# Sums of two weight slots in one operation and in place, six plain slots, a fourth weight buffer and a new order

## The chip, the cores and the metric

The kernel runs on 1 core of one Trainium2 chip. The metric is device microseconds of one execution. Engines: PE (TensorE, the matmuls; PEld is its weight load), DVE (VectorE), ACT (ScalarE), POOL (GpSimd), SP (SyncE, which here issues almost all DMAs).

## What is computed

A gated feed-forward block, for 4 sequences of 1024 tokens of width 512, with 2048 hidden rows and a down projection with weights of three values:

```python
scale = cond @ norm_w.T + 1.0
ms = jnp.mean(x * x, axis=-1, keepdims=True)
h = x * (scale[:, None, :] * jax.lax.rsqrt(ms + EPS))
u = h @ up_w.T
val, gate = jnp.split(u, 2, axis=-1)
h = val * jax.nn.gelu(gate, approximate=False)
hq = act_quant(h)          # 8 bits by row
wq = weight_quant(down_w)  # -1, 0, 1 by one scale
return hq @ wq.T + x
```

## The kernel before

**Tiles.** A batch is one sequence; its 2048 hidden rows are 16 slots of 128 rows of value and 128 of gate, and its 1024 tokens are two halves of 512. The f32 product of the up projection is made of f16: weights and activations are each split into a high and a low part, and high by high, high by low and low by high are summed in PSUM. A matmul is 128x128 by 128x512.

**Two forms of a slot.** A plain slot (`plain`, `plain_half`, and `plain_first` for the first half of slot 0) is value and gate, two halves of tokens, four blocks of 128 of the width, three terms: 48 matmuls. The other form (`slot` and `product`) takes the weights of a slot as 2x2 blocks, a11 and a12 of the gate, a21 and a22 of the value, 128x256 each, and the activations likewise, and makes seven products of six matmuls (Winograd's form of Strassen's): 42. It needs sums of the weights' blocks, and DVE and ACT add the products up (L868 to L907). In batches 1 to 3 all slots have this form. In batch 0 `SEVEN` says from which slot on: slots 0 to 6 are plain, 7 to 15 by products.

**The weights.** `w_load(j)` loads the f32 rows of slot j into a buffer of the large array H that `W_SLOT` names; in batch 0's later part three buffers (14, 12, 13) take turns. `w_range` and `w_scale` (L474, L476) scale them by powers of two. `w_rows` casts a high part (ACT, L499) and a low part (DVE, L500) of f16 and turns them by DMA. `s_sums(j)` makes the four sums of blocks (L526 to L529) into a place of their own, `sf`, which is H's buffer 17; POOL does this for the first slots and DVE for the later ones. `s_high` (L539) and `s_low` (L543) cast the sums, and `s_spill` writes all parts of the slot to `s_dram`.

**Batches 1 to 3** read the parts back into a ring of slots (SXY) by `s_load_x` and `s_load_y`: plain loads (L570) where batch 0 had turned all parts before it spilled them, and loads that transpose (L568) for the slots below `SEVEN`. `PLACE` says where each of a slot's seven parts stands.

**The start.** Two loads of x (L1130) bring the first 512 tokens. `first_sum` makes sums of squares (L1143 on ACT, L1145 on DVE), `first_root` their inverse roots, `first_scale` scales the rows (L1162, L1164), PE turns them into four banks of PSUM (`first_turn`, L1169: po_97, po_101, po_102 and A_91), and `first_high` (L1173 on ACT) and `first_low` (L1177 on DVE) make the high and low parts of x. The first weights are turned on PE as well (L484), into E_103 (one half of the rows), E_98 and then po_101 and po_102, and cast by L509 to L521. `keep_warm` (L1185) fills PE with matmuls that nobody reads. Squares go into junk buffers; the first one goes into the buffer of slot 0's value weights (`wn(0)`), whose load waits for it.

**What sets the order.** The functions only record steps. `Book.emit` issues them in the order of `ORDER`, a packed table of all steps that was planned beforehand; each engine runs its steps in that order, and waits at semaphores. The table holds one order for all five engines, SP's queue of DMAs among them.

Of the kernel before, what the change touches and what calls it, by code (L numbers as in the profile page):

```python
# [13 lines left out]
F16 = mybir.dt.float16  # L14
# [9 lines left out]
P = 128  # L24
# [12 lines left out]
PLACE = {4: 0, 5: 1, 6: 2, 2: 3, 3: 4, 0: 5, 1: 6}  # L37
# [35 lines left out]
class Book:  # L73
# [29 lines left out]
    'c-mcB2Y40b5}i#j1V|{UKnOh`AWcA2qzQsb5wU><MHEGv=(8fI=tD(CY@nz#dj~A2s7O&kB%vcBAU&az0MfGa&YAz;oA~zol6&vo',  # L103
    '-M`G7Idf+A#!DsnM^9)C*`bx>u%6Phq`Dl@Ku+s16{#k>HAxcXfTl~nhFS&Jq)T*^l@rQ8kt(tZW9;?c)sX`IORGsaDaP1)HAfEV',
    'Z(3REW41MVj#R)k+jR%t9oNm;1fP#;MOh`aFw#D)D?jN4_$EmL`AgHJBK|)o4{A1MN|ZPWb#&bL;&j=iTQR~(O_iVZLitnAmNU9b',
    '<D{od)C$r<j$v-@W4$()PV$3}kpbEocNJsC19}jjpVBiJbq7|yQw#Mn*`!4nvyaThnS3oL9c8k%kYVzgay7}=MI3fi9u^xUZ`#g_',
    'Gz0TA#5V!fbp$r-CLifVvKVt$k}}vq7Iu0Bdq0G|<>2!lN(&`PBRLDUEwWF;<tx2Zrfa6G*E+Z|Q@+rivJAUujBoSwJ$**H$_Shj',
    '`3@^7(gsqfH6>M+W8Ru_P4H~U`5WSFh&^u8suB-tEWkQn!ajK1CU59KsU=fz)nP3o_2h3|jFtX_I}X5x4ROab{ahv~eKtwjVr4f<',
    '6P&#l?=F^0qzzV(fsu-&hu$q$;4Bd%u+)CNL%xCKI8PRA`K)fl4tirQfnTn{4vu3LPvUivc9!>Wwk@ukti2=~))CpFyRp*sc7Kk1',
    'ua{t#T<<MF#uCldmB2)j+%8kGFCsDrqw>l|*z+K)Bn@krXzTnA_wsmJ9?%~0rS=Qn5Bd41{w^JKr?vvND@rq<HNtQ@P&){#_}0$U',  # L110
    '2X-C_{;_)|N<H8zMHXp$e3~NH!&^P&79EORUo5}l`d8&Hl|aKHtqt6+z?l|7UYIV;v5xMr2uJB83xMWdl&}1&2n1HZtSR_zqcl*i',
    ';CEp6sHR)|?6terNGoMrr2wh*Y@I!2pmxCLclCOF`pcgci=;$&&mAlDT+G-T{#gsZo@3|Q%agW)TGB@U126un^ifq<w!O5I&-8Y9',
    'U4ZqUFyC+5M$SiEFEAfv0v+Fg2g(E0uVTg&87H$eA9!}N(HC{#y-~25$Z<njBlxk0EJbuQm#VTyS7|ex&6fGVYzBDYGrbbH-LG8f',
    '^Lh`ydrt2~RJ4`Ru<mM20spka+PcC=1sJsr)<jlF!@7R8dC!9dGhnkCwuTS&S{qm71HBHPc~v#U#5Vm0c6k;%K82Yd1?~h9w+2!F',
# [12 lines left out]
    '`N0kP4$gFzHQ_nIOdTNgbrU{MN8C4;l^TYhY2Sd^hdUw4sOcQ<Qioh9V*K)ju@FaI0&d@L`R#W@ri=EDng=eb<aUM(5UruE#d0}Z',
    'odJul#{WbptqiH7TZrmY^UgY>%pmQ(u5fV>WfFeQ56cAH)5C~Y&ag=n;7uMIfzcw*W<0h*K?$<cUoi!+0`D4G_9n0Gv)6V&KN0WL',
    '`Dv`>05atVSm_tg2#vvDE{l?tm_z^8TKMCg35ahhx&qUE9N{=n&MZ+8df;yR*7+<2ag*%r=u{!E+O4bww&>e>BSyRk49}7F0eu-B',
    '6O6Zb=nZ!`Pw<ab0{`|P$IJ<@!19ZsB*@$!A=edRuIL~_ocF#$Y*Sem=^lL_t7A5-59@6}G{W*wgQ*h5cf5QjotgKgFIcRMIP5(o',  # L130
    'S85(+`6s3i$miX`r*C1EJQ6LwmV$SYk>pZbmx|RaKwO<4yW<3EizpWp2P5=F8Hg<2-(q1Nl>TDFQCH-_ESVuU+m+K0#R9~<1@%-0',
    'vB=|h=+#kBwhm>qhf_M640n&pW2Pt>8$)z5xIGUZ%rh$$K<l=YXY_vQ4IWr;@myetEKsti$dAyhwZU`Ff=}s#(B=K{_bs%?-?9C_',
    'j~q$0SVl4|KgA<+5Q{bCaUE+&p}z-#VVLioU3g@I^%C*Q6}W@ku}i55oK-l+7-ZX~h8A~@>Z+q$q>Js2_fU;)(s8EsiOn1JZJga~',
    '*vSV6bKN40@C3_4laY}&Tjuys%A0<<2i&m4W)z%Bv6{1nc`+Mn5!fLcx`j2b)0JBh4|_c}({!I<s;y~oSLI%%pWs|Ya96y|AlUhv',
    'R>QD@;&BVCM=ob(ZKHq3Fi{S;?IErbOVT3dMDT|@nC(yLquBdOb$fL7K{cWEf_NyotNoR$p_-{SE{Db>4q1J3ohLoh6A3pU%WO49',
    'As<yUPNClx7I%mnswZ`-uu7#`A~M{H#a2e;OLV%*KH2!<Pg8f?(fRtT<xR2tahq;IMMaGF(CL~MxcZhereYPFQCIW6>%d@{xZB0e',
    'UU2SqWxnOeWbbMc)jI;6BEgGFl`%|TwljA@0iQsmufeDfLko<uv*V!P>tRO$Y(!MwtTRf26|2}{48j;lg&mTly6%c`lvqYz3>*E8',
    'wO6%@;FM--uCRJYK%Q-`D{W20Rx9~jnR$<BCbGEG8dMb`pB0~qyB6O~^=o%p#OeCW5#i0`-$y55ymfX_jI8A97U&Mt$?nLq%vQtf',
# [1614 lines left out]
```

## Time and profile before

| | us |
|---|---|
| median of 3 runs | 717.09 (716.98 to 717.37) |
| the profiled execution | 716.0 |
| its span in the profile | 714.2 |
| PE busy | 707.6 |
| DVE busy | 527.8 |
| ACT busy | 432.8 |
| POOL busy | 144.2 |

The span goes from the first instruction to the last; 1.8 us lie around it. The profile's views give busy time of an engine by line and by stretch, waits with the engine that ended them, the chain of work that ended last, and for DMAs the time from issue to landing. A row such as `PE A L791 x12` is twelve matmuls in a row from line 791 into the PSUM tile A. Lines are those of the kernel before; after the change the same code stands 1 line earlier up to L430, and up to 11 lines later from L500 on (L791 becomes L802, L1177 becomes L1188, L570 becomes L581).

### The profile page before, as it was taken

To read this page: it belongs to the slowest core of one execution; us is meant where nothing else is said; L and a number is where in the kernel's file an instruction comes from. 1 tells how busy PE (TensorE), PEld (TensorE's weight loads), DVE (VectorE), ACT (ScalarE), POOL (GpSimd) and SP (SyncE) were. 2 spreads that over 40 slices of the span, in tenths; PEclk is the share of its full clock that TensorE was granted. 3 is DMA by queue.
4 is the path that set the end of the run, shared out by engine and by line. 5 is a ranking of instruction groups with operands and counts; after the bars stand their busy time and mean duration, and the time that the engine had idled before them with its cause. 6 is when DMAs were issued, how large, how long until landed. Compare 5 with 4: busy or idle time off the path is not lost.

```text
span 714.2 us, 10170 instructions
## 1 busy us (share of the span) xinstructions
PE 707.6 (99%) x3642; PEld 357.5 (50%) x3642; DVE 527.8 (74%) x837; ACT 432.8 (61%) x739; POOL 144.2 (20%) x161
## 2 busy tenths in 40 slices
PE   8999999999999999999999999999999999999998
PEld 4544444444444446655444455555444444444854
DVE  7968899998478896767659756775638846547895
ACT  5688889886578675654547476453434565334362
POOL 3675521120200005440202032800110000000010
PEclk9999999999999999999999999999999999999999
DMA  8778999999899973777345754566344354433324
GB/s 291 237 223 221 232 230 275 230 190 228 260 212 238 248 238 92 231 165 152 99 133 121 153 142 123 155 171 120 72 137 159 82 132 98 110 118 111 120 87 165
DMA packets 182943, 121.46 MB, mean 170 GB/s; under 512 B 144598, under 2 KB 150503, under 8 KB 182892
## 3 DMA queue, kind: packets, MB, share of 16 engines
q1 hardware_dynamic: 182346, 120.68, 64.8%
q8 instruction: 28, 0.46, 0.2%
q14 instruction: 23, 0.19, 0.1%
q10 hardware_dynamic: 546, 0.13, 0.1%
HBM read 63.73 MB, written 23.11 MB: 122 GB/s over the span
## 4 chain that ended last, share of the span: by engine, by line
PE 98%; DVE 2%; issue 0%
PE A L791 41%; PE E L791 21%; PE B L791 10%; PE po L1077 9%; PE E L806 5%; PE A L806 3%; PE B L806 2%; PE po L1027 2%; PE E L1027 1%; PE B L1077 1%; PE A L1027 1%; PE A L1185 1%; DVE wam L447 0%; PE E L1077 0%; PE A L1077 0%; PE B L1027 0%
## 5 line engine op out<-in xcount | busy, mean ns | idle before, releaser
L791 PEld LDWEIGHTS <-SXY 128*128 128x128 f16 x2226 | 217.7, 98 | 247.7 <-issue 0.2
L791 PE MATMUL A<-R,SXY 128*128 128x512 f16 x1200 | 291.0, 379 | 0.0
L791 PE MATMUL E<-R,SXY 128*128 128x512 f16 x600 | 152.5, 379 | 0.0
L923 ACT ACTIVATE gm<-H 128x512 f32<-128x512 f32 x120 | 75.6, 630 | 56.0 <-DVE R L924 45.3
L924 DVE TENSOR_TENSOR R<-R,gm 128x512 f32<-128x512 f32 x120 | 85.7, 714 | 29.1 <-ACT gm L923 28.5
L868 DVE TENSOR_TENSOR E<-A,v 128x512 f32<-128x512 f32 x57 | 39.7, 697 | 60.6 <-PE A L791 51.6
L791 PE MATMUL B<-R,SXY 128*128 128x512 f16 x318 | 82.7, 379 | 0.0
L1004 DVE TENSOR_TENSOR H<-H,am 128x1024 int8<-128x1024 f32 x64 | 77.0, 1222 | 0.0
L1009 ACT CAST R<-H 128x1024 bf16<-128x1024 int8 x64 | 65.3, 1042 | 18.1 <-DVE H L1004 17.9
L942 POOL PARTITION_ALL_REDUCE am<-R x8 | 15.6, 1950 | 256.8 <-DVE R L924 256.8
L1077 PE MATMUL po<-wd,R 128*128 128x256 fp8e4 x448 | 63.2, 273 | 0.0
L885 ACT ACTIVATE t<-B,sg 128x512 f32<-128x512 f32 x57 | 38.9, 682 | 36.2 <-PE B L791 36.1
L876 ACT COPY B<-A 128x512 f32<-128x512 f32 x57 | 32.8, 576 | 44.5 <-PE A L791 37.8
L1077 PEld LDWEIGHTS <-R 128*128 128x128 bf16 (+1 forms) x512 | 50.1, 98 | 18.7
L888 DVE SCALAR_TENSOR_TENSOR H<-A,sg,t 128x512 f32<-128x512 f32 x57 | 42.5, 746 | 20.7 <-PE A L791 19.8
L904 DVE TENSOR_TENSOR v<-A,v 128x512 f32<-128x512 f32 x57 | 39.1, 686 | 22.1 <-PE A L791 21.8
L901 ACT ACTIVATE t<-E,sg 128x512 f32<-128x512 f32 x57 | 38.7, 681 | 24.4 <-PE E L791 24.4
L907 DVE SCALAR_TENSOR_TENSOR H<-v,sg,t 128x512 f32<-128x512 f32 x57 | 45.2, 794 | 8.1 <-ACT t L901 8.0
L880 ACT COPY v<-E 128x512 f32<-128x512 f32 x57 | 33.2, 582 | 19.9 <-PE E L791 12.8
L806 PEld LDWEIGHTS <-SXY 128*128 128x128 f16 x216 | 21.0, 98 | 24.7 <-issue 0.3
L655 POOL TENSOR_SCALAR ssq<-ssq 128x2 f32<-128x2 f32 x12 | 4.2, 349 | 143.0 <-ACT xt L684 109.2
L1118 DVE SCALAR_TENSOR_TENSOR xr<-po,dq,xr 128x256 f32<-128x256 f32 (+1 forms) x36 | 21.8, 608 | 9.9 <-PE po L1077 4.4
(286 smaller groups left out, 864.1 us busy)
## 6 DMA issues: line engine op xcount, KB each, us to landing
SXY<-s_dram SPq DMA_DIRECT2D x63, 256.0 KB, 3.3
SXY<-s_dram SPq DMA_DIRECT2D x21, 384.0 KB, 3.4
H<-in_L_cond_up_w_dram SPq DMA_DIRECT2D x13, 512.0 KB, 4.8
s_dram<-SXY SPq DMA_DIRECT2D x6, 896.0 KB, 5.7
xr<-in_x_dram SPq DMA_DIRECT2D x19, 256.0 KB, 3.8
out_dram<-xr SPq DMA_DIRECT2D x19, 256.0 KB, 3.2
H<-in_x_dram SPq DMA_DIRECT2D x8, 512.0 KB, 5.1
s_dram<-SXY SPq DMA_DIRECT2D x10, 384.0 KB, 5.1
```

What stands on the lines that cost most here:

```text
L791: PE.matmul(o, s[:, w, k, :], xs(l, k), start=start and n == 0, stop=stop and n == len(TERMS) - 1, skip_group_check=True,)
L806: PE.matmul(ps, a[k // 2][:, w, k % 2, :], XP[:, l, k, h * TOK : (h + 1) * TOK], start=n == 0, stop=n == len(terms) - 1,)
L868: DVE.tensor_tensor(cur["E"], cur["A"], cur["v"], ALU.add)
L885: ACT.activation(cur["t1"], pb, AF.Gelu, scale=gain(g, 1))
L888: DVE.scalar_tensor_tensor(h_half(g - 1, 0), prev["A"], gain(g - 1, 0), prev["t1"], ALU.mult, ALU.mult)
L904: DVE.tensor_tensor(cur["v"], cur["A"], cur["v"], ALU.add)
L907: DVE.scalar_tensor_tensor(h_half(g - 1, 1), prev["v"], gain(g - 1, 0), prev["t2"], ALU.mult, ALU.mult)
L923: ACT.activation(gm, v, AF.Abs)
L924: DVE.tensor_tensor(m, m, gm, ALU.max)
L1004: DVE.tensor_tensor(whole(v), v, r.to_broadcast([P, 2, TOK]), ALU.mult)
L1009: ACT.copy(q, by_tile(whole(v)))
L1077: PE.matmul(po, w[:, j], m, start=start and j == 0, stop=stop and j == n - 1, skip_group_check=True,)
```

## The change

`s_sums` runs on every second slot, for two slots at once, and writes each sum over a block that is no longer needed; `w_cast` (taken out of `w_rows`) makes the f16 copies of the plain weights before that. `SEVEN` falls from 7 to 6, so that slot 6 of batch 0 is made by seven products and spilled already turned. H's buffer 17, free now, becomes a fourth buffer of weights, and `PLACE` moves three parts of a slot. The first square goes into another buffer. `ORDER` is a new table.

```diff
-PLACE = {4: 0, 5: 1, 6: 2, 2: 3, 3: 4, 0: 5, 1: 6}
+PLACE = {6: 0, 4: 1, 5: 2, 2: 3, 3: 4, 0: 5, 1: 6}
 ORDER = (
...
 )
-    W_SLOT = [14, 12, 13, 8, 9, 10, 14, 12, 13] + 3 * [14, 12, 13]
+    W_SLOT = [14, 12, 13, 8, 9, 10] + 3 * [17, 14, 12, 13]
-    sf = H[:, 17].rearrange("p t (n f) -> p (t n) f", n=2)
+    def sf(j):
+        return wn(j).rearrange("p t (n f) -> p (t n) f", n=2)
-    SEVEN = 7
+    SEVEN = 6
+    cast = set()
+    def w_cast(j):
+        cast.add(j)
+        n = H[:, 15 + j % 2].bitcast(F16).rearrange("p t (n w f) -> p (t n) w f", n=2, w=2)
+        a = 0 if j < SEVEN else 1
+        ACT.copy(n[:, a:, 0], sf(j)[:, a:])
+        DVE.tensor_tensor(n[:, a:, 1], sf(j)[:, a:], n[:, a:, 0], ALU.subtract)
     def w_rows(j):
+        if j not in cast:
+            w_cast(j)
         v = H[:, 15 + j % 2].bitcast(F16).rearrange("p t d -> p (t d)")
-        n = v.rearrange("p (n w f) -> p n w f", n=4, w=2)
-        f = wn(j).rearrange("p t (n f) -> p (t n) f", n=2)
         a = 0 if j < SEVEN else 1
-        ACT.copy(n[:, a:, 0], f[:, a:])
-        DVE.tensor_tensor(n[:, a:, 1], f[:, a:], n[:, a:, 0], ALU.subtract)
     def s_sums(j):
-        v = wn(j).rearrange("p t (n f) -> p t n f", n=2)
-        a11, a12, a21, a22 = v[:, 1, 0], v[:, 1, 1], v[:, 0, 0], v[:, 0, 1]
-        (POOL if j < 4 else DVE).tensor_tensor(sf[:, 0], a21, a22, ALU.add)
-        (POOL if j < 4 else DVE).tensor_tensor(sf[:, 2], a11, a21, ALU.subtract)
-        (POOL if j < 6 else DVE).tensor_tensor(sf[:, 1], sf[:, 0], a11, ALU.subtract)
-        (POOL if j < 6 else DVE).tensor_tensor(sf[:, 3], a12, sf[:, 1], ALU.subtract)
+        c = sorted(W_SLOT[n] for n in (j, j + 1))
+        v = H[:, c[0] : c[1] + 1 : c[1] - c[0]].rearrange("p s t (n f) -> p s t n f", n=2)
+        a11, a12, a21, a22 = v[:, :, 1, 0], v[:, :, 1, 1], v[:, :, 0, 0], v[:, :, 0, 1]
+        eng = POOL if j < 4 else DVE
+        eng.tensor_tensor(a22, a21, a22, ALU.add)
+        eng.tensor_tensor(a21, a11, a21, ALU.subtract)
+        eng.tensor_tensor(a11, a22, a11, ALU.subtract)
+        eng.tensor_tensor(a12, a12, a11, ALU.subtract)
     def first_sum(n, eng=ACT):
         if n == 0:
-            j = wn(0)[:, 0]
+            j = H[:, 0, 0]
     def first_batch(j, sc):
-        if n < NJ:
-            s_sums(n)
...
-        if n < NJ:
-            s_all(n)
         if j + 3 < NJ:
             w_scale(j + 3)
             if j < SEVEN:
                 w_rows(j + 3)
+            elif j % 2 == 0:
+                w_cast(j + 3)
+        if j % 2 == 0 and n < NJ:
+            s_sums(n)
+        if n < NJ:
+            s_all(n)
```

The new table moves steps in many places; two are shown. The first is DVE's queue in the first 21 us, from the last factors of the weights' scaling to the low parts of x; E_103 and E_98 are PSUM tiles with turned weights, po_97, po_101, po_102 and A_91 those with turned x. Before:

```order
L457 RECIPROCAL iv_106<-sw 128x2
L454 TENSOR_SCALAR sw<-wam_99 128x2
L509 CAST SXY<-E_103 128x2x256
L457 RECIPROCAL iv_105<-sw 128x2
L518 TENSOR_TENSOR SXY<-E_103,SXY 128x2x256
L1177 SCALAR_TENSOR_TENSOR R<-po_101,scT,R 128x512
L1177 SCALAR_TENSOR_TENSOR R<-po_102,scT,R 128x512
L1177 SCALAR_TENSOR_TENSOR R<-po_97,scT,R 128x512
L520 TENSOR_TENSOR SXY<-E_98,SXY 128x256
L1145 SCALAR_TENSOR_TENSOR R,ssq_0_88<-H 128x512 x2
```

And after:

```order
L457 RECIPROCAL iv_105<-sw 128x2
L1156 SCALAR_TENSOR_TENSOR R,ssq_0_88<-H 128x512
L1188 SCALAR_TENSOR_TENSOR R<-po_102,scT,R 128x512
L517 CAST SXY<-E_103 128x2x256
L1156 SCALAR_TENSOR_TENSOR R,ssq_0_88<-H 128x512
L528 TENSOR_TENSOR SXY<-E_98,SXY 128x256
L529 TENSOR_TENSOR SXY<-E_98,SXY 128x256
L526 TENSOR_TENSOR SXY<-E_103,SXY 128x2x256
L1188 SCALAR_TENSOR_TENSOR R<-po_97,scT,R 128x512
L666 TENSOR_SCALAR ssq_0_88<-ssq_0_88 128x4
L463 TENSOR_SCALAR sg_79<-sw,dx 128x2
L1188 SCALAR_TENSOR_TENSOR R<-po_101,scT,R 128x512
```

The two sums of squares of the second token half (L1145, now L1156) and the low part of po_102 moved ahead; the low part of po_101, which was the first of the low parts, is now behind nine of these rows. PE puts further transposes of weights into po_101 (and into po_102) once DVE has read them. PE's own first products are now of the value half, into A_94, where they were of the gate half, into B_92.

The second place is SP's queue early in batch 1, some 225 to 250 us into the span: loads of slots' parts into SXY (4x128 and 12x128 are the transposing ones), transposes of the down projection's weights (wd) and loads of them (nx, xn, xt). Before:

```order
L602 DMA nx_122<-in_L_cond_down_w_dram 128x1024
L570 DMA SXY<-s_dram 128x1024
L568 DMA_TRANSPOSE SXY<-s_dram 128x12x128
L628 DMA_TRANSPOSE wd<-xr_84 128x8x128
L602 DMA xn_114<-in_L_cond_down_w_dram 128x1024
L628 DMA_TRANSPOSE wd<-xr_83 128x8x128
L570 DMA SXY<-s_dram 128x1024
L568 DMA_TRANSPOSE SXY<-s_dram 128x4x128
L570 DMA SXY<-s_dram 128x1536
L570 DMA SXY<-s_dram 128x1024
L414 DMA sc_113<-rows_dram 128x4x128
L570 DMA SXY<-s_dram 128x512
```

And after:

```order
L579 DMA_TRANSPOSE SXY<-s_dram 128x12x128
L581 DMA SXY<-s_dram 128x1024
L613 DMA xn_114<-in_L_cond_down_w_dram 128x1024
L581 DMA SXY<-s_dram 128x1024
L581 DMA SXY<-s_dram 128x512
L613 DMA nx_124<-in_L_cond_down_w_dram 128x1024
L581 DMA SXY<-s_dram 128x1536
L613 DMA xt_115<-in_L_cond_down_w_dram 128x1024
L639 DMA_TRANSPOSE wd<-xr_84 128x8x128
L581 DMA SXY<-s_dram 128x1024
L581 DMA SXY<-s_dram 128x1536
L579 DMA_TRANSPOSE SXY<-s_dram 128x4x128
```

The loads of SXY now stand later against PE's rows, with more loads of the down projection's weights between them, and each is issued nearer to its first use.

More of the change, by code (lines that the diff above doesn't have):

```diff
@@ new lines @@
+    'V{_Ew2s+!-c#NYy$<dy~SiY)Ub#NW(<2m_57UF)%p%i<$maWwIPFX2Cr5|MpC{r>uUMM~AjEuv}GMKVmNd07EgUsNl$K_Fsl-Dtl',
+    '8rp6)+a;s$k;w*Xf3NJ9qoSU)0_RhzRdO@sOrSQlNpHMJ34wp(LAe-HXyJUWWr=jg3mDFId@M~k%5Kz_eW)6f{SvMzSE|q>fNuDm',
+    'I?JKIMaSdR<s@qAXK9Nr9AD2JKqY&>6DfE_KLrwkSBKyYu6CDM<xg2Cw{zusUqgCwMZ72HqY9egdpSnGPQU`BNPE6Nh86OI%)wQ(',
+    ';8@BHq%%rt1joX|e7X~s+88fUzHVH>d(y~Obq0x2&3yG046_&jCUUKF>3yB#bF4>6`txz5Qs=`t|1|lYI$wiUHkw8o@DyH>zvU^)',
+    'U4h?b&?lat<=>#M<}gCkd)MI>N_{_HFTzjur0Vu+%%;Yl$HUaAdRh~_EA5~@atlTv!8F*4_ufRi?ziZEm%5-IBi+XR-K?n|))Buk',
@@ new lines @@
+    's($4dJLo?X(4V%^Pe6M-N(<V`i3|7BGoHo-8Lir9#9YJoaq<K@bHzL5Dq3(N?E@^t-Li#G4WnIFqcuMj%5c19<1D64hVWBQIBy0t',
+    'CV<N@pRX#Vo?9w?81c^b{i*NM^1BSRxZ#X=g1Y(JK0k#Q_&!fAM<x#1nPKQ6v*@YAoKNt`#9LBCzaK%{>-WQwfj(Tx9FC*kb9l{J',
+    '_c<AfQH);wyf&;6l*4WEKJEI7jk8d$<+F-Kr5KNjdrrcM@;9H1JhhdV`%z-gw{it$8oE^H8O4%Ca#j?*3W!}AbHJ_mKs0KAJZkVa',
+    '@3l8_lufjzqM=6rPOg6-BMeZ_K2QFH;;TNlnpgpP^nO{-r`8kcOnSyQa2ID++`SH;^R)r;!~J~K<0Hna#d_E=$mO;3>HT$OJ37k}',
+    'JKvG`S<Za%Z|Yio>%W|@5|ZgL>O~cBh}buq(k1cgddBS+)DG|vV>6pbRgE}%gpwVR!<1{OJWCWgBZ|-MWI3hl%;<rSF;J5wh~n)G',
@@ new lines @@
+    'Bg#|eOX04~l*??*?P9uKNR(<rYy?z~ugQHnBK32c_+JW&teS&hv)ARE1u{jRhx+1q_`~K``@A8q@mgaW8)lhgbfq7BEkpS2WqE+F',
+    'Q{-+e7QMTb-E%;`q{S3pcFOrOhM$`8`O_R>F;N@1hu?lCHo!F2L4IfUIV@`#MK$?eAkNe46O~n)J7fT3HjnvrtbBl?qTPvkVNa|i',
+    '4*etP7%dZc*8}o06c=^2G8jNac8AKXtIR|%`~D8Kwu3&rl5>0@w=$X@ke_(I7Cxm1=`o2J?GO533&z}Zd6;WC6*dZX(4tM4bN-U%',
+    'xYINV^k%%~h*~@H<VLh|Be->)r0=_En=JRz$|X^mxmG=L1m^(#u~7EVo3A!38F#ivLKdU?PFx}1^11z@Ub>sJ?d8ge=`x;YyK{_B',
+    'h>73JBeKS1*cu+Bq#flquLrfyGGesFJ9SZDETt`Or?oOrhwJVpyD)_7(#({>QEo+DX0?FdALH4R)b(`!XUhhj`AKe<zwjH!-xb!7',
@@ new lines @@
+    'xq<Uajgb}9L@j6*{f|dK)r`w{8d1%mv3AIqjXNaVMsEz|A1P<?;t);I;Sjy+AYU!k!khU(Vc0e(Be}F&GoHIyJ|fy5qE63P{DPj_',
+    '%-*-rSB{9oL}g8r!V!GBdC~Ty3|>7c8FJV(phr1ARh=F)Smq%@Hbt>Jq4;>Me4%_uifE%Il>2q&x374nh&lZo8N^Jt*t|^-jr#<~',
+    'R604stG1SZq@8TSy)xM%v639XO=Jdc4&@%D<Rs>WlQEZ{^QEE`dKL*vu4s46)~@TT$oHX4&L7(MI&y^mTZs~GmWDi|EFvAs8Yx+r',
+    '6zJM6kp-4r9Y*w$L2^ydOXlKAO6es2PI{V$sBG>~&!-2<4~(lWcE&}cj=kD4mCC+I`kF-xq&+dTfO#;-=Fq&;m&o6jnV=KD&nNOI',
+    '8hz(ktKuEF!nz`~L8jqBB`?c<V$uftq<Yh6aI4vD(UL|@9O8G?hw3(k?Cg|mq&MlYiLnJ{h02WTMIMcs(q8I=u$&h8#a`)b66tY>',
@@ new lines @@
+    'sH!;r73Iw(S6T0$JjJ+bq3l2&M1*WG-VWmOLx$9<@1~aTE@vd`>n3VJF--pt+S)*jt4%h&HI~(S<7@Idcgz<3zJ}4P@vJ!l#ET}T',
+    'xxKQ0xg*uzS&3Q-5RaEX<rY47lw+$GIo{+l{w8Wp?~dkE1gcLiug8RNba2R9fbolqM1A~eYCp-(q=-8c19|>)*^)G@XdNvAZzHw#',
+    '0$MXVCK5MJP~VklA6JzeW8VBkoF!EIBQc&USwY4%gpt(BVg;DXRUD)gW#F(pSH8g@W~yq`;xy)YMZzR#{Haf=XN)5=FGKEegZI%N',
+    'EU)cm-JqGFwPi77TzxFo)i#;b0U0%U_j^Rq>0zg!p3kfLs{T<6KN`2zm1#anAye$fYDGOxnWb`P=fS{@@`>rZsiC<>rNg>q<csU5',
+    '0cVvYdfqIeRV1OtUn%DKs>Yfd(K2h9Nz-h$mExl8B0m4TOh<qDnDaYU8AaW8%e#iC<iE-~_L2?2M?1*P#~3%COiu75s~6>=9qjom',
@@ new lines @@
+    'V);?g`}9mEC0AdZNp8>wN4#ew^G{Jhb6`!b-f0KSj;rl`G@17we7~4_QckQfGvBOV7;d4h%A2n^?x+~t(pZ6VrdrGj7t3={H0~nr',
+    'VGjM>d9HFJWdRAq_bWX=T^x4hrTX5d?!;~31%dMU#f->2W~-*AF-68R^z5JLOLL_cIs3nT4g9Ly&uGmw1Sv;E)Vy>NbNvD-Bgg!x',
+    '!^v&?kjo}Z4x;?mC2SbH9YZ~>K{YO~mf6O&<FV#+o<x}kbIy{`$_W@ju3p+RQGK?y*|-$fzk=*Zqv|FocE87r4OHYx8hHMv#|g%b',
+    'zK@b;IDd1lbsSkhTaQQ;ViD#dX`}Zkcl=0hJ4YfUX+&oFwdmZ+*j%n1B=0cR)LU1RK`MXRECcwuHLM@F{Cf}Cu~wWK(b|n@#Qc;k',
+    'XDm}_J)vy6i1pPK=Brc4f>zO6G*hS^^r*x9dpw3Q8|6Z>F}0^w{#UUch>jMNsvXyHw|R9GPYxB=Glz7yZ)d_p4{R42F9oy?o<=76',
@@ new lines @@
+    'FJu^K6@D+`z55+fSH!!R+Wi|L*Q1T+OT`b>PLhqGS-|byxZlei^*tF^??+tZcJC<>`#(snFK1lLh#`AJzh9`F;UZcw)AB)YNj|5i',
+    'c2Ek)_y^c-oBmEv=NN4D`>U*eKUJp5DzU39Ci=DF(@kT~?vZQB0-v$noo(`HI4Q`s*i50XAF&wR!N}b%t}=0l<F&(W_r}#S#u!**',
+    '46+@OM9Q;GTE%|J<&O4bb@@cl-^J}<x#MGUX7%ctX0>FCp9I5`RN_`ETU!mZmwTv*&1N56g|pik`t@jXn<lJE=kwX4GS?9CE~}c`',
+    ';x2KY5-bLC7=QPgy$YE(P7qNRFj7jOp`lts;?!2}Z?z0(no%#^ET)tEE_+SdC6zT$q5TenwIRL!sC2YmVK#lVwc+-qNM!Yzj3g<d',
+    '*G!UW#<-KMm$g;2qRRGb|Bd6cwkyjSLEX9blAPrau1K*rUvk2%!0q>y_D}3KW>MPnV~xNQT=BWl7iWP{uNn9sJA0fD',
@@ L1350, in glu_quant_kernel @@
     w_load(4)
-    s_sums(0)
     w_range(3)
@@ L1373, in glu_quant_kernel @@
     w_rows(4)
+    s_sums(2)
     s_all(2)
-    s_sums(3)
     w_load(6)
```

133 lines of the change are left out of this document (48 added, 85 removed).

## The prediction

> **What bounds the kernel now.** I read the page's totals first, then busy time by stretches, then the waits of TensorE (PE) and of the chain that ended last.
>
> ```profile
> span 714.2 us, 10170 instructions
> PE 707.6 (99%) x3642; PEld 357.5 (50%) x3642; DVE 527.8 (74%) x837; ACT 432.8 (61%) x739; POOL 144.2 (20%) x161
> ...
> PE 98%; DVE 2%; issue 0%
> ```
>
> PE is busy 99% of the span, and 98% of the chain that ended last is PE. The next view is the same busy time by stretch; after a stretch's length, the columns are PE, weight loads, DVE, ACT, POOL, then granted clock, DMA share and GB/s.
>
> ```profile
> 24.00:60.00 36.00, 35.98 (x176) 17.42 (x175) 27.32 (x48) 26.18 (x51) 26.69 (x37) 1.00 0.84 250
> 60.00:150.00 90.00, 90.00 (x419) 40.80 (x418) 83.71 (x147) 78.53 (x143) 30.69 (x33) 1.00 0.96 229
> 150.00:320.00 170.00, 170.00 (x881) 86.12 (x880) 128.32 (x184) 113.71 (x191) 32.43 (x35) 1.00 0.84 213
> 320.00:640.00 320.00, 320.00 (x1622) 158.55 (x1621) 209.52 (x299) 166.49 (x279) 40.06 (x39) 1.00 0.50 127
> ```
>
> From 24 to 640 us PE has no visible gap, at a granted clock of 1.00. So time can leave this kernel in two ways only: fewer or shorter matmuls, or an earlier start. It can come in where PE starts to wait. All waits that the view of PE's waits lists now (microseconds, times, longest) lie in the first 18 us:
>
> ```profile
> PE A L1185 <- DVE H L268: 1.2, 1, 1.2
> PE A L377 <- DVE mx L370: 1.1, 1, 1.1
> PE B L849 <- DVE SXY L509: 0.2, 1, 0.2
> PE po L1169 <- DMA H<-in_L_cond_up_w_dram: 0.2, 1, 0.2
> PE E L484 <- POOL H L476: 0.2, 1, 0.2
> ```
>
> What a matmul of 128x512 costs in a saturated stretch is read from one row of the chain: twelve in a row take 2.59 us, so one takes 0.216.
>
> ```profile
> 149.72 2.59 PE A L791 x12
> ```
>
> **Part 1: six matmuls fewer.** Slot 6 of batch 0 changes from 48 matmuls (plain) to 42 (seven products of six). On PE's order the count of 128x512 matmuls falls by exactly 6: 12 more into A, 6 fewer into B, 12 fewer into E. 6 x 0.216 = **-1.30 us**, all of it on the path, because PE is saturated there (the stretch 60 to 150).
>
> **Part 2: the sums of weights.** Before, the ones of a 128x256 operand are 44 on DVE and 20 on POOL; afterwards there are 24 on DVE and 8 on POOL, of 128x2x256.
>
> ```profile
> L526 DVE TENSOR_TENSOR H<-H x12: 397/416/929, 49.1 to 146.6; 128x256 f32<-128x256 f32 x12
> ...
> L526 POOL TENSOR_TENSOR H<-H x4: 727/728/1587, 14.2 to 40.5; 128x256 f32<-128x256 f32 x4
> ...
> L868 DVE TENSOR_TENSOR E<-A,v 128x512 f32<-128x512 f32 x57 | 39.7, 697 | 60.6 <-PE A L791 51.6
> ```
>
> DVE: 44 x 0.416 = 18.3 us. An operation of the new size has its like in L868 at 0.697: 24 x 0.697 = 16.7, so 1.6 us less. Slot 6 by products needs two more DVE operations of 128x512, some 1.5 us, so DVE's sum is about unchanged. POOL: 20 x 0.728 = 14.6 us before; for the new size no row exists, and I take twice 0.728 (bounds 0.73, if width were free, and 1.59, the longest row): 8 x 1.46 = 11.7. None of this is on PE's path: it is hidden by PE's matmuls, and DVE keeps 6.3 idle us in 60 to 150. I cost it at **0**. If the cover went, the most would be the 1.5 us of slot 6's additions. The copies that w_cast makes are the ones w_rows made before, issued earlier: 0, under the same cover. The fourth buffer lets weight loads start earlier, which no PE wait after 18 us asks for: 0.
>
> **Part 3: the first 21 us.** The new order changes what stands ahead of the first products.
>
> ```profile
> 7.76 0.63 ACT L1143 ACTIVATE R<-H 128x512 f32<-128x512 f32 x1
> ...
> 13.45 1.22 DVE L447 TENSOR_REDUCE wam<-H 128x2 f32<-128x1024 f32 x1
> ...
> 15.13 0.68 DVE L509 CAST SXY<-E 128x512 f16<-128x512 f32 x1
> ...
> 15.84 0.69 DVE L518 TENSOR_TENSOR SXY<-E,SXY 128x512 f16<-128x512 f32 x1
> 16.45 2.06 DVE L1177 SCALAR_TENSOR_TENSOR R<-po,scT,R 128x512 f16<-128x512 f32 x3
> 18.43 0.41 DVE L520 TENSOR_TENSOR SXY<-E,SXY 128x256 f16<-128x256 f32 x1
> 18.76 0.68 DVE L1145 SCALAR_TENSOR_TENSOR R<-H 128x512 f32<-128x512 f32 x1
> ...
> 19.37 0.69 DVE L1145 SCALAR_TENSOR_TENSOR R<-H 128x512 f32<-128x512 f32 x1
> ```
>
> DVE runs without a break here, one row every 0.6 to 0.7 us, and the cast at 15.13 releases the first product:
>
> ```profile
> 15.87 1.76 PE L849 MATMUL B<-R,SXY 128*128 128x512 f16 x6 [0.23 <-DVE SXY L509]
> 17.47 0.83 PE L484 MATMUL po<-ident,H 128*128 128x128 f32 x4
> 18.14 0.59 PE L849 MATMUL B<-R,SXY 128*128 128x512 f16 x2
> 18.57 0.60 PE L484 MATMUL po<-ident,H 128*128 128x128 f32 x4
> 19.00 1.46 PE L849 MATMUL A<-R,SXY 128*128 128x512 f16 x6
> ```
>
> From 19.00 on PE never waits again for long; by then it has done all 16 transposes of the first weights (L484) and 8 products. In the new order DVE has, behind the same reductions (which end their small rows at 15.05 by the rows' places): a sum of squares of the second token half (0.61 from row to row), the low part of po_102 (0.67), the cast (0.65), a second sum of squares (0.61), two low parts of 128x256 (2 x 0.33, as 18.43 to 18.76), the low part of E_103 (0.61), that of po_97 (0.67), two small rows (0.25) and the low part of po_101 (0.67). That is 5.40 us, so it ends at 20.45. PE must put weights' transposes into po_101 and waits for that row: it starts them at about 20.5, and after two of them (0.11 each: the four from 18.57 reach to 19.00) goes on with products at 20.77. By then it has done 14 of the 16 transposes and 15 products, that is 7 x 0.216 - 2 x 0.109 = 1.29 us more than before at 19.00. The start is worse by 20.77 - 19.00 - 1.29 = **+0.48 us**.
>
> Bounds. In the new program two of ACT's three squares read the second load of x. The next two answers are SP's issues of x and their landing.
>
> ```profile
> 1.22 1.01 SPq L1130 DMA_DIRECT2D H<-in_x_dram  x2
> ```
>
> ```profile
> DMA to landing us min/median/max: 6.0/6.6/7.2
> ```
>
> The second issue is at about 1.7, and at the shortest landing of 6.0 it is there at 7.7, just ahead of the square at 7.76. If it lands some 0.6 us sooner, the ACT and DVE rows up to the reductions move by as much, and the term is -0.14. If DVE's rows begin later by one more sum of squares (0.61), it is +1.1. I take +0.48.
>
> **Part 4: the order of transfers.** In batches 1 to 3 PE reads slots' parts back from memory by SP's queue. A load can start when PE has read its buffer the last time, and must land before the next use. Counted on PE's order, for the pieces of SP's queue shown above in the section on the change: between last reader and first use stood, before, 59, 54, 48, 77, 48, 52 and 62 matmuls (in the order of the seven loads of SXY there); after, 27 (the 12-block transpose), 38, 75, 60, 24 (the 384 KB load), 41, 45 and 29 (the 4-block transpose). So 27 x 0.216 = 5.83 us, 24 x 0.216 = 5.18 us, and 29 x 0.216 less two DMA issues ahead of it. The next two answers are for the lines of transposing and plain loads in 200 to 250 us.
>
> ```profile
> L568 SPq DMA_TRANSPOSE SXY<-s_dram x10: 1195/1736/4524, 199.0 to 246.0; - x10
> ...
> DMA to landing us min/median/max: 3.6/5.7/7.2
> ```
>
> ```profile
> L570 SPq DMA_DIRECT2D SXY<-s_dram x12: 327/460/692, 206.5 to 248.9; - x12
> ...
> DMA to landing us min/median/max: 2.8/3.8/6.5
> ```
>
> Two issues are 0.92, so the third margin is 5.34. At the medians (5.7, 3.8) only the transposes are near: at a median landing the 4-block one comes 0.36 late, the others in time. At the longest landings the three are late by 1.37, 1.32 and 1.86, in sum 4.5, at the shortest by 0. Elsewhere the least margin is 28 matmuls less one issue before (5.59), and 23 less one issue after (4.5, a 128 KB load at some 407 us, where DMA is busy half the time, not 0.84).
>
> ```profile
> SXY<-s_dram SPq DMA_DIRECT2D x63, 256.0 KB, 3.3
> ```
>
> A plain load's usual 3.3 us is within 4.5. Bounds 0 and 4.5; nearest to the medians: **+0.3 us**.
>
> The Trainium skill's "DMA: Bandwidth & Descriptors", section "Latency and other measured facts", has the fixed part of a transfer grow from 0.2 us of memory latency to 2 us at high load. The trace agrees that the busy stretch is slower (3.8 there against 3.3 over the run); by the rule alone late loads would be likelier at 230 to 245 us than at 407.
>
> **The sum.** -1.30 + 0 + 0.48 + 0.3 = -0.5 us. The profiled execution took 716.0 us, 1.8 around its span of 714.2; it would come to 715.5. The median of the runs is 717.09, 1.1 above that execution, so I forecast 717.09 - 0.5 = **716.6 us**. 0.2% is 1.43 us, about what a measurement of this kernel can tell from no change: below 715.66 is faster, above 718.52 slower.
>
> **The rivals.**
>
> *The early start and loads in time.* The second load of x lands early, no transfer is late, and one of PE's short waits for weights (0.2) goes: -1.30 - 0.14 - 0.2 = -1.64: **715.5 us**. For it: the load of weights that waited for ACT's first square (buffer of the first weights) no longer does, so the turns of the weights can be done sooner. Against: DVE's rows, not the weights, pace 12 to 16 us. 0.24.
>
> *Late loads decide.* One mechanism: loads of slots' parts in 225 to 245 us land after PE wants them. It decides from 718.52 - (717.09 - 1.30 + 0.48) = 2.25 us of stalls, that is when two of the three come at their longest landing (1.86 + 1.32 or more): 3.2 us gives **719.5 us**. For it: margins fell from 48 matmuls to 24 to 29 while transfers of weights of 512 KB still run between them. Against: of the 22 loads of that stretch half the transposes took under 5.7 and half the plain ones under 3.8 us, and two at their longest are wanted. 0.12.
>
> *POOL's longer operations hold DVE.* In 24 to 60 us POOL is busy for 26.69 of 36 us, and L526 on DVE took 0.929 once where 0.416 is usual, so the engines disturb each other. A hold of up to 1.46 in place of 0.73 for each of 8 sums, and PE waiting for the evictions behind it by 0.1 to 0.2 each, as its two short waits of 0.2 are: 8 x 0.15 = 1.2, giving **717.8 us**. Against: it's fewer POOL microseconds in all. 0.06.
>
> The Trainium skill's "SBUF — State Buffer", section "SBUF: two separate sides", says that a DVE operation with two operands in SBUF and GpSimd share a port pair as a lock held for the whole instruction. It speaks against this change, and the 0.929 agrees; by it this rival would happen at each meeting.
>
> *The change doesn't do what it says* (slot 6 stays plain): the order's counts exclude it.
>
> **Chances.** Forecast 0.58 (within 0.2%), early start 0.24 (faster), late loads 0.12 (slower), POOL 0.06 (within 0.2%). Faster 0.24, same 0.64, slower 0.12. The range reaches down into the early start (715.2) and up to where late loads begin to decide (718.5): about 0.1 is left out on each side.
>
> **What would show it.** Part 1: 42 matmuls where slot 6's 48 stood. Part 3: PE's last wait behind DVE's low part of po_101 near 20.5 us, and products from 20.8. Part 4: waits of PE for SXY<-s_dram near 230 to 245 us, 0 to 0.5 us each; none there, and the forecast is 0.3 too high. Part 2: no PE wait for POOL or DVE between 24 and 150 us. The prediction is wrong if PE waits on batch 0's sums, or starts continuous work before 20.2 or after 21.4 us.

## The result, and the profile after

| kernel | median us | lowest to highest | runs |
|---|---|---|---|
| before | 717.04 | 716.44 to 717.37 | 4 |
| after | 739.16 | 736.32 to 740.0 | 4 |

The change makes the kernel slower by a ratio of 1.0303 (95% interval 1.0274 to 1.0331). The forecast was 716.6, within 0.2%. The page of the changed kernel, whose profiled execution took 739.46 us (line numbers are from here on those of the changed kernel):

```profile
span 737.3 us, 10072 instructions
...
PE 715.7 (97%) x3636; PEld 360.8 (49%) x3636; DVE 527.9 (72%) x819; ACT 435.2 (59%) x740; POOL 136.7 (19%) x148
...
PE 88%; DMA 5%; DVE 3%; ACT 1%; issue 1%; SPq 0%; DVEq 0%; ACTq 0%
```

PE has six records fewer (3642 before), and DVE's sum is where it was (527.8 before). But the span is 23.1 us longer, PE's busy time is 8.1 us longer with fewer matmuls, and the chain that ended last, 98% PE before, now has DMA, DVE and ACT in it. These are PE's waits, all of them:

```profile
PE A L802 <- DVE H L899: 5.1, 2, 4.4
PE A L802 <- DVE v L915: 4.8, 1, 4.8
PE E L817 <- DVE H L845: 3.9, 1, 3.9
PE E L363 <- DMA H<-in_cond_dram: 1.7, 1, 1.7
PE A L1196 <- DVE H L269: 1.2, 1, 1.2
PE A L376 <- DVE eps L1133: 1.1, 1, 1.1
```

The last two were there before. New are three long waits for DVE and one for a DMA at the start; the second wait that the first row counts is a short one of 0.7 us. Next comes busy time by stretch (PE first, then PEld, DVE, ACT, POOL, granted clock, DMA share, GB/s), cut around the long waits:

```profile
8.00:12.00 4.00, 2.32 (x12) 1.61 (x11) 2.94 (x18) 3.22 (x8) 0.69 (x1) 0.87 0.98 356
12.00:18.00 6.00, 6.00 (x29) 5.48 (x28) 4.70 (x15) 3.14 (x6) 3.08 (x4) 0.52 0.80 297
...
24.00:70.00 46.00, 46.00 (x225) 22.06 (x223) 39.80 (x64) 35.35 (x67) 28.16 (x29) 1.00 0.86 231
70.00:80.00 10.00, 6.09 (x22) 2.38 (x21) 7.39 (x10) 4.49 (x7) 3.76 (x3) 0.83 0.39 56
80.00:114.00 34.00, 34.00 (x159) 15.46 (x158) 27.44 (x41) 28.87 (x52) 11.66 (x11) 1.00 1.02 251
114.00:125.00 11.00, 6.64 (x24) 2.59 (x23) 6.30 (x9) 5.48 (x11) 3.25 (x2) 0.84 0.66 157
125.00:163.00 38.00, 38.00 (x178) 17.19 (x176) 29.39 (x54) 30.25 (x54) 5.99 (x12) 1.00 0.99 244
163.00:175.00 12.00, 7.16 (x22) 2.53 (x21) 8.17 (x13) 6.39 (x12) 3.69 (x4) 0.72 0.52 103
175.00:320.00 145.00, 144.19 (x728) 70.99 (x727) 110.50 (x154) 98.86 (x164) 23.45 (x27) 1.00 0.87 216
320.00:640.00 320.00, 320.00 (x1649) 161.21 (x1648) 213.00 (x306) 170.15 (x286) 44.77 (x47) 1.00 0.52 130
```

Nearly all of the loss lies before 175 us. Between the long waits PE is saturated as before, and from 175 us on nearly so. In each of the three stretches with a wait the granted clock is below 1. The rows of PE around the last one show both parts of the price:

```profile
163.35 1.03 PE L802 MATMUL B<-R,SXY 128*128 128x512 f16 x4
169.21 2.72 PE L802 MATMUL A<-wd,SXY 128*128 128x512 f16 x6 [4.84 <-DVE v L915]
171.72 2.77 PE L802 MATMUL A<-xr,SXY 128*128 128x512 f16 x6
174.28 1.08 PE L802 MATMUL A<-R 128*128 128x512 f16 x3
```

Six matmuls take 2.7 us where six at 0.216 would take 1.3: after the wait PE runs at half speed, some 0.43 us per matmul, and behind 174 us it is back. Counted from the starts of matmuls, each due 0.216 us behind the one before it (0.109 for a narrow one), the 23.1 us come to: six matmuls fewer, -1.3; the start, +3.1; the three pauses, 4.1 + 4.5 + 5.0 = +13.6; the slow matmuls behind them, 1.4 + 1.6 + 2.7 = +5.7; smaller pauses after 175 us, +1.1, of them 0.9 at 230 us; small rests in batch 0 and the tail behind the last matmul, +0.9. The start's +3.1 is that of these two executions: the one before took 716.0 us, 1.0 less than its median, and the medians lie 22.1 us apart, so in medians the start is, by estimate, nearer +2.

What held DVE is read from its own queue. These are its rows around the second pause:

```profile
109.75 0.69 DVE L537 TENSOR_TENSOR H<-H 128x512 f32<-128x512 f32 x1
110.48 0.69 DVE L538 TENSOR_TENSOR H<-H 128x512 f32<-128x512 f32 x1
111.20 0.69 DVE L539 TENSOR_TENSOR H<-H 128x512 f32<-128x512 f32 x1
117.13 0.69 DVE L540 TENSOR_TENSOR H<-H 128x512 f32<-128x512 f32 x1 [5.24 <-DMA SXY<-H]
```

Three of the four sums of a pair of slots run back to back, and the fourth waits 5.24 us for a DMA that writes SXY and reads H. That is the transposing DMA of `w_rows` (L509). The view of that line names the three rows that waited for it, and nobody else:

```profile
who waited for it (us, times):
  DVE H L537: 6.2, 1
  DVE H L540: 5.2, 1
  DVE H L539: 4.7, 1
...
DMA to landing us min/median/max: 3.7/4.8/7.6
```

The DMA reads the f16 copies of a slot in a buffer of their own; the sums neither read nor write them. The program as built gives the places, in words of f32 within a partition of H, and DVE's row at 117.13 has an explicit wait for a DMA ahead of it; among the 24 sums on DVE only the three that waited have one:

```
DVE L540 at 117.13 us writes 15104 to 15359 (buffer 14) and 18176 to 18431 (buffer 17)
SP  L509 at 111.96 us reads  15616 to 16383 (buffer 15)
```

The new form of `s_sums` reaches both buffers of a pair with one stride. For slots 6 and 7, 10 and 11, 14 and 15 the pair is 14 and 17, and the buffers 15 and 16, from which the transposing DMAs read, lie between. Nothing overlaps, but the sum has a wait on that DMA all the same, where the DMA stands ahead of it in the order table. **Theory A**: the program's tracking of accesses takes the span of the strided access, from 14 to 17, for the access. Rivals: the transfers are simply too slow for the new order (B), or POOL's longer sums hold DVE (C).

### The profile page after: what moved, and what is told of

Its sections match the earlier page's. It is cut to its first block, busy times and chain, and to the rows that moved or that the text cites. A ratio compares the mean times of both kernels' runs of the same rounds, so it can differ in the third digit from the quotient of the medians.

```text
span 737.3 us, 10072 instructions
## 1 busy us (share of the span) xinstructions
PE 715.7 (97%) x3636; PEld 360.8 (49%) x3636; DVE 527.9 (72%) x819; ACT 435.2 (59%) x740; POOL 136.7 (19%) x148
## 4 chain that ended last, share of the span: by engine, by line
PE 88%; DMA 5%; DVE 3%; ACT 1%; issue 1%; SPq 0%; DVEq 0%; ACTq 0%
PE A L802 39%; PE E L802 19%; PE B L802 10%; PE po L1088 8%; PE E L817 2%; PE po L1038 2%; DMA SXY<-H 1%; PE A L817 1%; DMA H<-in_cond_dram 1%; DMA s_dram<-SXY 1%; DMA R<-H 1%; PE E L1038 1%; PE B L1088 1%; PE A L1038 1%; DMA SXY<-s_dram 1%
## 5 line engine op out<-in xcount | busy, mean ns | idle before, releaser
L802 PE MATMUL A<-R,SXY 128*128 128x512 f16 x1212 | 295.1, 380 | 5.1 <-DVE H L899 5.1
L802 PE MATMUL E<-R,SXY 128*128 128x512 f16 x606 | 157.4, 379 | 0.1
L802 PEld LDWEIGHTS <-R 128*128 128x128 f16 x168 | 16.9, 101 | 21.3 <-issue 2.5
```

Of the source, the lines that this page charges most:

```text
L802: PE.matmul(o, s[:, w, k, :], xs(l, k), start=start and n == 0, stop=stop and n == len(TERMS) - 1, skip_group_check=True,)
```

## The experiments

**The buffers apart.** The copies go to 16 and 17 and the fourth weight buffer to 15, so that pairs are neighbours; the order table is the same.

```diff
-    W_SLOT = [14, 12, 13, 8, 9, 10] + 3 * [17, 14, 12, 13]
+    W_SLOT = [14, 12, 13, 8, 9, 10] + 3 * [15, 14, 12, 13]
-        n = H[:, 15 + j % 2].bitcast(F16)
+        n = H[:, 16 + j % 2].bitcast(F16)
-        v = H[:, 15 + j % 2].bitcast(F16)
+        v = H[:, 16 + j % 2].bitcast(F16)
```

> The changed kernel, with the f16 copies in buffers 16 and 17 and the fourth buffer of weights at 15 (before: copies 15 and 16, weights 17), so that no pair of weight buffers has a copy buffer between them; the order table is unchanged. Theory A (the sums' pair of buffers 14 and 17 reaches across 15 and 16, the program takes that for an overlap, and DVE's sum waits for the transposing DMA that reads 15): the three DVE waits of 4.7, 5.2 and 6.3 us go, with them the three PE stalls of 4.1, 4.5 and 5.0 us and the slow matmuls behind them, 19.6 us together: 719.5 us (717 to 722); the start stays as late as it is. Rival B (these transfers are simply slow, or their data are needed): 739 us, the waits only change their line. Rival C (POOL's longer sums hold DVE): 739 us, as POOL's sums stay.

Measured: 719.73 us (718.97 to 722.18), 19.4 less than the change. In the same view of the transposing DMAs nobody waits for them, though they land no sooner (median 5.0 us), and the four sums of the second pair run on:

```profile
who waited for it (us, times):
busy tenths in 40 slices 0000000000000000000000000000000000000000
DMA to landing us min/median/max: 3.7/5.0/7.3
```

```profile
106.65 0.69 DVE L538 TENSOR_TENSOR H<-H 128x512 f32<-128x512 f32 x1
107.38 0.69 DVE L539 TENSOR_TENSOR H<-H 128x512 f32<-128x512 f32 x1
108.10 0.69 DVE L540 TENSOR_TENSOR H<-H 128x512 f32<-128x512 f32 x1
```

B and C fall: the transfers are no faster, and POOL's eight sums take 11.2 us in both kernels. Theory A had forecast 719.5. The profiled execution was the slowest of the six (722.18), which matters for its start, below.

**The DMAs recorded later.** Buffers as in the change; three steps of the order table go behind the sums (a fourth moves along, so that SP's queue keeps its order). Every engine's own order is the same, only the recorded place against DVE's differs.

```diff
+        order.insert(591, order.pop(581)); order.insert(892, order.pop(889))
+        order.insert(1244, order.pop(1240)); order.insert(1243, order.pop(1223))
```

> The changed kernel, with three transposing DMAs recorded some steps later in the table, behind the four sums of the pair that they stand in; every engine's and every queue's own order stays as it is, and so do the buffers. Theory A: the waits turn round, the DMA waits for the sums and DVE no longer for the DMA; 719.5 us (718 to 722), up to 1 us more than with the buffers apart, since the DMAs start later. Rival B (slow transfers): later DMAs make it slower than 739. Rival C (POOL holds DVE): 739.

Measured: 719.37 us (718.53 to 721.96), 19.8 less than the change. The waits turned round as theory A has it. In the view of SP's waits the DMA's line now waits three times for the last sum, 8.6 us in all, which it never did in the changed kernel:

```profile
SPq L509 <- DVE H L540: 8.6, 3, 3.7
```

So the wait comes from what the program recorded, not from what the data need: with the sums first, the same DMAs, sums and buffers no longer hold PE up.

**One of the three.** Only the last pair of those moves (1240 and 1223).

> The changed kernel with only the last of the three transposing DMAs recorded behind the sums. Theory A, each wait with a price of its own: the stall of 5.0 us at 164 and the 13 slow matmuls behind it (2.8 us) go, the other two stay: 739.2 - 7.8 = 731.4 us (730 to 733). If the waits were one delay handed on, so that work caught up elsewhere: less than 4 us gained.

Measured: 731.85 us (730.48 to 732.3), 7.3 less than the change. The view of the DMA's line has two waiting rows left (5.3 and 4.7 us). Each wait has its own price, and work behind it is not caught up.

**The start: the load of the conditioning first.** With some 19.5 us explained, the start (+3.1) is left. PE waited 1.7 us for the second load of the conditioning, and the clock fell.

```diff
+        order.insert(2, order.pop(26))
```

> The changed kernel, with the second load of the conditioning issued right behind the first on ACT's queue, 2 us earlier. Theory S (PE waits 1.7 us for that load at 10.84, the granted clock falls to 0.5 from 12 to 17 us, and this is what makes the start 3.1 us later than before): the wait goes, the clock stays 1.0, 2 to 3 us less: 736.5 us, and first products near 17 us. Rival X (the second load of x, landed 0.6 us later than before because the weights' loads run beside it, sets the start): 738.5 us or more, clock still low.

Measured: 738.85 us (736.74 to 740.38), no clear gain; theory S was not confirmed. PE no longer waits for that load, but in this execution the first load of x landed late: ACT's first square began at 7.50 us, not 5.93. (Over the profiles of this study that load lands between 5.3 and 7.5 us, so one of them can't say whether the edit did it.) The clock in 12 to 16 us was 0.71 (0.50 in the change).

**The junk back in its place.**

```diff
-            j = H[:, 0, 0]
+            j = wn(0)[:, 0]
```

> The changed kernel, with the first square's junk put back into the buffer of slot 0's value weights, so that their load waits for the square as before. Rival X (weights' loads beside the second load of x make it late): x lands 0.6 us earlier, the start gains 0.6 to 2 us, 737.5 us. Theory S: the weights come later, nothing gained, 739 to 740 us.

Measured: 740.34 us (738.73 to 740.89). It tells nothing of rival X: the new table has the load ahead of the square, so the load waited for nothing, and the square overwrote slot 0's value weights.

**Eight matmuls that nobody reads**, on the kernel with the buffers apart, ahead of the PE row that waits.

```diff
+        order[82:82] = [order[65]] * 8
```

> The kernel with the buffers apart (719.7), with eight matmuls that nobody reads put ahead of the PE row that waits for the second load of the conditioning. Theory W (PE stands idle from about 8.9 to 10.8 us, the granted clock falls to 0.5 for some 6 us, and the 24 transposes of x and weights behind it take 0.213 instead of 0.109 us each, 2.5 us in all): the clock stays near 1.0 from 12 to 18 us, first products 2 to 2.5 us earlier, 717.4 us. Rival X (the second load of x and what follows on ACT and DVE sets the start; the slow transposes are hidden behind it): the clock rises and the time stays, 719.5 us.

Measured: 718.43 us (717.64 to 719.64), 1.3 less than without them, about half of what theory W forecast. The two ratios to the kernel before have intervals that touch (1.0014 to 1.0033 here, 1.0029 to 1.0065 there), so the size is uncertain; a second pair, below, gives 0.9. In its profile the start is 0.4 us later than in the kernel before. The stretch from 12 to 16 us, of the kernel with the buffers apart and then of this one:

```profile
12.00:16.00 4.00, 3.60 (x17) 3.15 (x18) 2.67 (x7) 1.92 (x3) 1.36 (x2) 0.51 1.00 333
```

```profile
12.00:16.00 4.00, 4.00 (x33) 3.30 (x31) 3.89 (x12) 3.01 (x7) 2.30 (x4) 1.00 1.04 392
```

At full clock PE gets through 33 matmuls there instead of 17, and DVE and ACT, which wait for its transposes, through 19 instead of 10 rows. The clock is the reading here; the counts overstate it, because these are the slowest execution of the one kernel (722.18) and the fastest of the other (717.64). In the kernel with the DMAs recorded later, profiled near its median (719.39), the same stretch has 24 matmuls and 16 rows of DVE and ACT, at a clock of 0.57.

**Weights' loads behind the first square**, as in the kernel before: the first of the new table's squares gets its junk in the value weights' buffer, and SP's loads are recorded behind it.

```diff
-        if n == 0:
-            j = H[:, 0, 0]
+        if n == 2:
+            j = wn(0)[:, 0]
...
+        order[21:47] = [s for s in order[21:47] if s.eng != "SP"] + [s for s in order[21:47] if s.eng == "SP"]
```

> The kernel with the buffers apart (719.7), with the first square's junk in the buffer of slot 0's value weights and that load recorded behind the square, so that the loads of weights wait for the square as in the kernel before. Rival X: the second load of x lands at 7.7 instead of 8.4 to 8.6 us, the conditioning's second load 1 to 2 us earlier (fewer loads ahead of it), PE waits less; 1 to 2.5 us gained, 717.5 to 718.7. Theory W alone: PE's idle gap before the conditioning shrinks only as far as that load comes earlier; the clock in 12 to 16 us says which.

Measured: 718.89 us (716.94 to 720.21), 0.8 less than with the buffers apart alone; the clock in 12 to 16 us was still 0.60. ACT's square of the second load of x began at 7.82 us, not 8.59, as rival X has it, but the time is just outside its range and the intervals of the two ratios touch (1.0011 to 1.0033, 1.0029 to 1.0065): this run doesn't decide on rival X. And with the eight matmuls:

> Both edits of the two runs beside it on the kernel with the buffers apart. If both count, 716.5 to 717.5 us; if only the clock does, as with the eight matmuls alone; if the weights' loads then come too late for the first products, above both.

Measured: 719.01 us (718.02 to 720.29), no better than either, so there is no sign that the gains add up. In its profile PE waited 1.2 us for a low part of x, on a queue of DVE that had waited twice, 1.2 us together, for loads of weights; but both loads of x were late in it as well (squares at 7.17 and 8.52 us, without this edit 5.58 and 7.47), so it isn't shown that the late weights are the reason.

**One load of down_w earlier.** With the eight matmuls one wait of PE is left after the start, 1.2 us near 209 us (in the change it was 0.9 us at 230):

```profile
PE A L802 <- DVE H L899: 1.2, 1, 1.2
```

Followed back, DVE waited for ACT, and ACT for a load of down_w that stands on SP's queue behind a read-back:

```diff
+        order.insert(1598, order.pop(1601))
```

> The kernel with the buffers apart and the eight unread matmuls (718.4), with one load of down_w put ahead of a read-back that holds SP's queue from 191 to 196.6 us. Theory L (that load, landed at 203, holds ACT, whose evictions behind it hold DVE's, and PE waits 1.2 us for the last of these near 209 us): PE's wait of 1.2 us goes, 1.3 us less, 717.1 us, as fast as the kernel before. Rival (ACT's and DVE's own work in that slot is too long): the wait stays, 718.4.

Measured: 717.23 us (716.07 to 718.83, before 716.94 beside it); that wait is gone from the list. The interval, 0.9992 to 1.0009, lies clear of that of the kernel without this edit. The load now goes out 4 us ahead of the read-back, and ACT found its data there:

```profile
193.72 0.33 SPq L613 DMA_DIRECT2D xt<-in_L_cond_down_w_dram  x1
197.78 0.33 SPq L981 DMA_DIRECT2D am<-am_dram  x1
```

**A sum of squares on DVE later**, on top of that.

```diff
+        order.insert(149, order.pop(138))
```

> The same, with the first of the two sums of squares on DVE put behind the low part of po_102 and the cast of E_103. If DVE's row is what the first product waits for, 0.3 to 0.6 us less than the run beside it: 716.6 us. If ACT's high parts set the start now (PE's row at 16.5 us waited for ACT), no change: 717.1.

Measured: 717.17 us (716.33 to 720.82), no change: at full clock DVE's sum of squares is not what the start waits for.

**A constant set earlier**, on the kernel at 717.23, and then the same without the eight matmuls.

```diff
+        order.insert(3, order.pop(23))
```

> The kernel of the run at 717.2 us (buffers apart, eight unread matmuls, one load of down_w earlier), with DVE's setting of a constant moved to the front of its queue; ACT's first activation waits for it, and behind that on ACT's queue stands the second load of the conditioning, issued at 3.52 us. It will be issued near 2.5 us and land 1 to 2 us sooner. If the start still hangs on it: 716.5 us. If ACT's high parts and DVE's rows set the start: 717.2, no change.

> The same without the eight unread matmuls. Theory W with the late load as what opens PE's gap: the load lands before PE wants it, the clock stays near 1.0 without the extra matmuls, 717 us. If PE has too little to do there in any case: the clock falls to 0.5 or 0.7 between 11 and 17 us all the same, and it takes 718 to 718.5 us.

Measured: 716.97 us (716.49 to 718.04) with them and 717.83 us (717.3 to 719.24) without; before 717.02 beside both. The load landed near 7 us in both, long before PE wanted it, and the clock in 12 to 16 us was 1.00 and 0.60. So the late load alone was not the reason of the low clock: without the extra matmuls PE had 2.62 busy us from 8 to 12 (4.00 with them), with a wait of 1.1 us, now for ACT. What the earlier load brings by itself, some tenths of a microsecond, these runs don't separate.

The best version, 716.97, is as fast as the kernel before (ratio 1.0001, interval 0.9993 to 1.001); none was clearly faster.

## Why the prediction was wrong, point by point

**Part 1, six matmuls fewer: right.** PE has 3636 records for 3642, and outside the pauses it stays saturated; -1.30 us are in the sum above.

**Part 2, "I cost it at 0": this step failed.** Its sizes were right: DVE's sums took 0.69 us (0.697 forecast), DVE's total is 527.9 for 527.8, and POOL's eight sums 11.2 us (11.7). What it left out is whom the operations wait for. It counted the in-place sums as work under PE's cover and looked for added waits of PE, of SP's queue and, as a rival, of DVE for POOL; on DVE's queue the change had added three waits for DMAs of 4.7, 5.2 and 6.2 us, with evictions queued behind them. "No PE wait for POOL or DVE between 24 and 150 us" was the test that the prediction set, and the profile after fails it. 13.6 us of pauses and 5.7 us of slow matmuls came of it; two experiments took back 19.4 and 19.8 us by removing these waits. That the waits are owed to the span of the strided access is shown: no byte is shared, they go when the span no longer covers the copies, and they turn round when the DMA is recorded behind the sum. The slow matmuls are a second thing that no term had: the prediction priced every matmul at 0.216, which holds only while the clock of 1.00 does.

**Part 3, the start: the sign was right, the size was not.** +3.1 us in the profile (by estimate some +2 in medians) instead of +0.48, beyond the bound of +1.1. The forecast took PE's transposes at 0.109 us, the clock of 1.00 that stood in the rows of before. In the new order the granted clock is 0.52 from 12 to 18 us, and DVE's cast, by the forecast's sum due at 16.3 us, waited for PE's transposes instead:

```profile
15.27 0.67 DVE L1156 SCALAR_TENSOR_TENSOR R<-H 128x512 f32<-128x512 f32 x1
...
19.02 0.69 DVE L517 CAST SXY<-E 128x512 f16<-128x512 f32 x1 [2.00 <-PE E L484]
```

The clock is one part. In all five profiles with the eight unread matmuls it was 1.00 in 12 to 16 us, and the start, counted as in the sum above, was 0.4, 0.7, 1.5, 1.7 and 2.1 us later than before; in the eight profiles without them it was 0.50 to 0.71, and the start 1.4 to 4.7 us later. Only the best two come near the forecast's own arithmetic. By the pair of medians the unread matmuls bring 0.9 us (716.97 against 717.83).

The second load of x looks like the other part. The bounds let it come only sooner, but in all thirteen profiles of the new order ACT waited for it, 0.6 to 2.6 us, and began its square at 7.47 to 8.87 us; the kernel before had no such wait, and its square began at 7.76. Among the five profiles at full clock the start is the later the later that square is (7.47, 8.29, 8.37, 8.52 and 8.77 us, in the order given). That is a comparison across different kernels, one execution each, and no run tests it alone, so how the rest of the start divides stays open.

**Part 4, the order of transfers: the mechanism was wrong, and that its size lay within the bounds of 0 and 4.5 was luck.** PE never waited visibly for a load of slots' parts in the changed kernel; of all profiles of the new order only that of the kernel with the later sum of squares shows such a wait, 0.2 us at 245. The pause that came (0.9 us at 230; 1.2 to 1.5 in the kernels without the long waits) was longer by two links: a load of down_w held ACT, ACT held DVE, and DVE held PE. Moving that one load took 1.2 us back. The 3.8 us that the prediction sets against 3.3 is of loads of several sizes; for those of 256 KB alone the view gives 3.6 in 200 to 250 us against 3.3 over the run.

**The rivals.** Late loads deciding, at 719.5, had the right side and the wrong mechanism. POOL's longer operations are excluded as the cause: they take the same 11.2 us in the two kernels that lose the pauses. The early start didn't come.

**The chances.** Slower had 0.12. All of it was put on one mechanism, late loads. The rival about POOL had the path of what came (DVE held, evictions late, PE waiting), but another cause, 1.2 us and a place within 0.2%; a wait of DVE for a DMA was not among the rivals at all.

## What to carry to other kernels

When an edit merges two tiles into one strided access, look at what lies between them: dependence tracking may take the whole span, and then any DMA on the tiles in between becomes a wait. Count the waits of every engine in the new program, not only those of the engine that bounds it, and for each new wait ask what evictions are queued behind it. A new order also has to keep PE busy before the first real work: the transposes there took 0.21 us instead of 0.11 while the granted clock was down.

## What the runs showed of the hardware

PE's clock halved behind pauses of 4.1, 4.5 and 5.0 us, for 7, 8 and 13 matmuls, which made such a pause a third to a half dearer; pauses of 0.9 to 1.5 us had no such price. In narrow stretches of the changed kernel's profile the granted clock is 0.51 from 75.8 to 79.2 us, 0.50 from 120.2 to 123.6 and 0.50 from 168.0 to 174.8, and 0.97 to 1.00 in the 0.8 us on either side. So the low clock lasted 3.4 us twice and 6.8 us once, and in two of the three it began before PE had work again. The Trainium skill's "TensorE: Matmul & The Clock Gate", section "Part 1: The HAM clock gate (the "warmup" mystery)", says that an idle window of some 3.4 us puts the array at half rate until it has been busy for about one window again. The long pauses and the first two low stretches agree; the third lasted two such windows.

The start is less plain: between 8.9 and 10.8 us PE stood idle 1.7 us at once and had 2.3 busy us in the four from 8 to 12, and the clock was at 0.50 from 11.0 to 17.8 us. In the kernel with the DMAs recorded later, whose first 24 us have the same steps, it was at 0.50 only from 12.4 to 15.8. The two starts, 3.1 and 2.0 us later than before, differ in the same direction.

The first load of x, issued at 1.2 us in every kernel, landed between 5.3 and 7.5 us from profile to profile, by when ACT's first square of it began. One execution therefore says little about a microsecond at the start: the kernel with the buffers apart ran from 718.97 to 722.18 us.
